# A 3x3 convolution in fp32 on one Trainium2 core: Winograd blocks of 2x2 outputs become blocks of 2x4, two images at a time

## The chip, the cores and the metric

The kernel runs on one core of a Trainium2 chip. The metric is the device time of one execution in microseconds. A core has a matrix engine (PE; its weight loads are listed apart, as PEld), a vector engine (DVE), a scalar engine (ACT), a general-purpose engine (POOL), and DMA queues that SP and POOL issue. Each engine works off its own list of instructions in order and waits for the others by semaphores.

## What is computed

The input x has 4 images of 1024 channels on a 32x32 grid (1024 positions), all fp32. Layer 0 is an attention block: q, k and v by 1024x1024 projections, rotary embedding and RMS norm of q and k, 16 heads of 64, softmax over the 1024 positions, an output projection, RMS norm, and the residual. Layer 1 is a bottleneck block, each batch norm over all 4 images and all positions of a channel:

```python
out = relu(bn(conv(x, w1, b1, 1, 0)))    # 1x1, 1024 -> 256
out = relu(bn(conv(out, w2, b2, 1, 1)))  # 3x3, 256 -> 256, pad 1
out = bn(conv(out, w3, b3, 1, 0))        # 1x1, 256 -> 1024
out = softplus(residual_scale)[0] * out
return relu(x + out)
```

The change concerns the 3x3 convolution, called conv2 here; its neighbours are conv1 and conv3.

## The kernel before

All four images are worked one after the other through projections and attention. Attention of an image goes by two chunks of 512 query positions and, in each, by eight pairs of heads. For a pair, PE computes eight score tiles (L789), ACT takes their exponentials (L796), DVE adds these up for the softmax's denominators (L815), PE multiplies them with v (L824), and ACT copies the context out (L830). Three PSUM banks hold scores. After the last pair come the denominators (L893, copied at L962, reciprocal at L963, sent through DRAM and multiplied into the contexts at L769, L770), then the output projection (L490, copied out at L544), whose weight chunks SP's queue loads into a ring of eight tiles.

Work of the next stage is slipped into the last attention chunk. `filters()` (L1145) turns the 3x3 filters into Winograd filters in a list of steps, and one step is issued after each head pair of that chunk, from the second pair on. On an engine's list a step so stands ahead of the next pair's exponentials and additions. Before the change the steps are the load, three sums along one direction, and two along the other (each with one ACT scaling of 1024 elements, L1166, between DVE operations L1165 to L1168). The 16 transformed filters stay in SBUF.

conv1 (L1013, and `conv1_first`/`conv1_rest`, L1054) is a 1x1 convolution. For images 0 to 2 it is done with a Strassen-like scheme in `conv1_rest`, a generator whose steps are interleaved by hand; for image 3 directly. Results go to DRAM (`h1d`), their statistics to `h1stats`, and `norm_of` (L1119 to L1126) makes scale and shift of the norm.

conv2 is a Winograd F(2x2, 3x3). A block of 2x2 outputs needs a 4x4 patch of inputs, transformed to 16 values; each of the 16 is multiplied over the channels, and four outputs come from them. So it has 16 products for 4 outputs, in place of 36. An image is loaded (`load_h1`, L1437), normed and clipped by ACT into a padded tile (`fill`, L1440), transformed by DVE across (`across`) and down (`down`, both L1451) into V tiles, multiplied by PE (`uv`, L1516, tiles of 256 blocks), copied in part by ACT (`copies`, L1531) and combined by DVE (`outputs`, L1539 to L1551) with bn_stats (L1553). The transform of the next image is interleaved with the products of this one. After the last image comes the norm of conv2 (L1558 on ACT, L1559 and L1560 on DVE). conv3's four weight tiles (`w3t`) and the residual x1 (`load_x1`) are loaded during conv2; conv3 is at L1656, with the copy L1667, statistics L1669, and the finish L1636 to L1640.

The order on PE, DVE, ACT and POOL is that of the program's lines, by hand; SP's queue of loads is ordered by the scheduler. PSUM banks, the V tiles, a ring of small work tiles (`temp`), one of larger ones (`big_temp`) and a ring of weight chunks (`chunk`) are shared, and an instruction that writes a shared buffer waits for its last reader.

Of the kernel before, what the change touches and what calls it, by code (L numbers as in the profile page):

```python
# [18 lines left out]
P = 128  # L19
B, C, H, W = 4, 1024, 32, 32  # L20
N = H * W
# [64 lines left out]
def program(ctx, tc, x, wblk, w2, w3, vecs, cos, sin, out, bad):  # L86
# [70 lines left out]
    wd2 = dram.tile([4, len(OUTER), len(SUMS), P, CH], F32, name=f"wd2{u}")  # L157
    dens = dram.tile([P, CH], F32, name=f"dens{u}")
# [4 lines left out]
    with tc.tile_pool(name=f"st{u}", bufs=2) as st, ExitStack() as s:  # L163
# [912 lines left out]
        def conv1_rest(b, ys, w, ss, t1, t2):  # L1076
# [13 lines left out]
            four(o, ss[2], lambda i: ys[:, i, half[1]], False, False)  # L1090
            h22 = temp(f"c22_{b}")
            nc.scalar.copy(h22, o)

            def done22():
                nc.vector.tensor_tensor(h22, h22, p5, ALU.add)
                keep_h1(b, 1, 1, h22)

            after(1, done22)
            product_done()
            yield  # L1100
            four(o2, ss[3], lambda i: ys[:, i + NH, half[1]], False, True)

            def done12():
                nc.vector.scalar_tensor_tensor(h12, o2, col("b1", 0), h12, ALU.add, ALU.add)
                keep_h1(b, 0, 1, h12)

            after(1, done12)
            product_done()
            yield
            four(o, w[1][1], lambda i: ys[:, i + NH, half[0]], False, True)  # L1110
# [36 lines left out]
        def filters():  # L1147
# [5 lines left out]
            def load():  # L1153
                for dy in range(3):
                    for dx, slot in enumerate((0, 1, 3)):
                        nc.gpsimd.dma_start(
                            raw[dy][:, slot, :].rearrange("p (c f) -> p c f", c=NPT), taps[:, :, 3 * dy + dx, :]
                        )

            steps.append(load)  # L1160
            two = [tp.tile([P, 2, CH], F32, tag=n, name=f"u2_{n}") for n in ("cos", "sin")]

            def sums_of(g0, g1, g2, new):

                nc.vector.tensor_tensor(new, g0, g2, ALU.add)  # L1165
                nc.scalar.mul(g1, g1, 0.5)  # L1166
                nc.vector.scalar_tensor_tensor(g1, new, 0.5, g1, ALU.mult, ALU.add)
                nc.vector.tensor_tensor(new, new, g1, ALU.subtract)  # L1168

            for dy in range(3):  # L1170
                r = raw[dy]
                steps.append(lambda r=r: sums_of(r[:, 0], r[:, 1], r[:, 3], r[:, 2]))
            for h in range(2):
                js = slice(2 * h, 2 * h + 2)
                steps.append(lambda h=h, js=js: sums_of(*(raw[dy][:, js] for dy in range(3)), two[h]))
            for i in range(4):
                for j in range(4):
                    uw[i, j] = two[j // 2][:, j % 2] if i == 2 else raw[(0, 1, None, 2)[i]][:, j]
# [218 lines left out]
        for b, nxt in ((1, 2), (2, 0), (0, None)):  # L1397
            steps = conv1_rest(b, back[b], w, ss, rows1, rows2)
            for _ in range(2):
                next(steps)  # L1400
            if nxt is not None:
# [10 lines left out]
        rest()  # L1412
# [11 lines left out]
        inner.close()  # L1424
        vp = s.enter_context(tc.tile_pool(name=f"vp{u}", bufs=1, reuse_waits="tile"))
        hx = s.enter_context(tc.tile_pool(name=f"hx{u}", bufs=3, reuse_waits="tile"))
        pad = [vp.tile([P, H + 2, W + 2], F32, name=f"pad{i}") for i in range(NPT)]
        cols = vp.tile([P, 4, H + 2, W // 2], F32, name="cols")
        for i in range(NPT):
            nc.gpsimd.memset(pad[i], 0.0)  # L1430
        TR, TC = H // 2, W // 2
        n1, n2, vt, h1, h2 = {}, {}, {}, {}, {}

        def load_h1(b):
            for i in range(NPT):
# [319 lines left out]
```

## Time and profile before

| | |
|---|---|
| median of 3 runs | 2645.34 us (2644.81 to 2646.97) |
| the profiled execution | 2645.64 us |
| its span, first to last instruction | 2643.8 us |
| PE busy | 2624.5 us (99%) |
| DVE busy | 2136.3 us (81%) |
| ACT busy | 1128.4 us (43%) |
| POOL busy | 451.9 us (17%) |
| granted PE clock | 0.998 |
| output projection of the last image begins | 2220.9 us |
| conv1 begins | 2305.6 us |
| conv2 begins | 2406.0 us |
| conv3 begins | 2518.4 us, its second half of channels (k=1) some 7.5 us later |
| last product of conv3 | 2628.8 us |

Positions are microseconds from the start of the span. A row of the groups names the line of the kernel, the engine, the operation, output and input with their shapes, and the count; then the busy time and the mean length of one in ns; then the idle time of the engine just ahead of these instructions and what ended it. A PE product in fp32 leaves two records. The records of operations that follow each other on an engine overlap a little, so a sum over many is made with the distance from start to start, which is less than the length.

### The profile page before, as it was taken

The page shows a single profiled execution, that of the slowest core. Times are in us where ns is not written, and L with a number is a line of the kernel's source. Part 1 is how long each engine was busy: PE and PEld are TensorE (multiplying, and loading weights), DVE is VectorE, ACT ScalarE, POOL GpSimd, SP SyncE. Part 2 cuts the span into 40 slices and gives each one's busy share as a digit, 9 for nine tenths or more (in the row PEclk, how much of TensorE's full clock was granted, in tenths as well). Part 3 has the DMA queues.
Part 4 walks back from the last instruction along what each step waited for, and adds up shares of the span by engine and source line. Part 5 has one row for each costly group of instructions (what it writes and reads, how often), then busy time and mean ns, then how long its engine had stood idle before and what let it go on. Part 6 is the DMA issues. An engine that isn't in the chain of part 4 may idle for free. (4 is left out here: it accounts for less than half of the span.)

```text
span 2643.8 us, 40486 instructions
## 1 busy us (share of the span) xinstructions
PE 2624.5 (99%) x15436; PEld 1628.9 (62%) x15436; DVE 2136.3 (81%) x2566; ACT 1128.4 (43%) x1586; POOL 451.9 (17%) x590
## 2 busy tenths in 40 slices
PE   9999999999999999999999999999999999999997
PEld 4448533488888333688886333888884335846843
DVE  5567899998887876888879777977988779877977
ACT  2222566533442565333343655233525654312266
POOL 2542323101011222100111222000111222010000
PEclk9999999999999999999999999999999999999999
DMA  8887888777667453557775551765774442683165
GB/s 287 288 257 202 240 262 258 209 219 237 188 183 210 88 94 64 150 172 225 190 198 144 97 90 46 219 202 177 194 212 90 84 105 84 206 278 104 64 236 210
DMA packets 252810, 466.81 MB, mean 177 GB/s; under 512 B 31808, under 2 KB 124784, under 8 KB 252608
## 3 DMA queue, kind: packets, MB, share of 16 engines
q1 hardware_dynamic: 195728, 287.80, 35.4%
q0 software_dynamic: 48816, 159.54, 24.6%
q10 hardware_dynamic: 8064, 16.78, 1.8%
q8 instruction: 125, 2.05, 0.3%
q14 instruction: 77, 0.63, 0.1%
HBM read 329.53 MB, written 97.01 MB: 161 GB/s over the span
## 5 line engine op out<-in xcount | busy, mean ns | idle before, releaser
L796 ACT ACTIVATE p<-sc 128x1024 f32<-128x1024 f32 x512 | 479.8, 1049 | 15.4 <-PE sc L789 15.1
L789 PE MATMUL sc<-q,k 64*64 64x512 f32 x4096 | 455.5, 591 | 0.0
L824 PE MATMUL cx<-p,to 64*64 64x512 f32 x3072 | 338.2, 589 | 0.0
L789 PEld LDWEIGHTS sc<-q,k 64*64 64x64 f32 x4096 | 149.7, 132 | 293.4 <-ACT p L796 148.0
L815 DVE TENSOR_TENSOR den<-den,p 128x1024 f32<-128x1024 f32 x192 | 237.9, 1239 | 21.9 <-ACT p L796 2.2
L815 DVE TENSOR_TENSOR den_T<-den_T,p 128x1024 f32<-128x1024 f32 x192 | 236.3, 1231 | 20.4 <-DVE den_T L815 1.4
L824 PEld LDWEIGHTS cx<-p,to 64*64 64x64 f32 x3072 | 117.5, 133 | 212.1 <-issue 211.0
L485 PE MATMUL p_v<-w_v,x 128*128 128x256 f32 x928 | 210.5, 379 | 1.7 <-DVE x L456 1.5
L490 PE MATMUL p_y<-q,w_y 128*128 128x256 f32 x928 | 210.6, 380 | 0.8 <-issue 0.8
L490 PEld LDWEIGHTS p_y<-q,w_y 128*128 128x128 f32 x928 | 175.7, 190 | 30.3 <-issue 5.8
L485 PEld LDWEIGHTS p_v<-w_v,x 128*128 128x128 f32 x928 | 176.0, 190 | 27.5 <-DVE x L456 2.8
L830 ACT COPY q<-cx 128x512 f32<-128x512 f32 x64 | 37.5, 585 | 341.1 <-PE cx L824 341.1
L490 PE MATMUL p_k<-to,w_k 128*128 128x256 f32 x672 | 152.2, 380 | 0.0
L490 PE MATMUL p_q<-to,w_q 128*128 128x256 f32 x672 | 152.2, 379 | 0.0
L490 PEld LDWEIGHTS p_k<-to,w_k 128*128 128x128 f32 x672 | 127.4, 190 | 18.4 <-issue 1.2
L490 PEld LDWEIGHTS p_q<-to,w_q 128*128 128x128 f32 x672 | 127.4, 190 | 18.4 <-issue 1.2
L770 POOL TENSOR_SCALAR q<-q,vec 128x512 f32<-128x512 f32 x42 | 80.5, 1926 | 215.6 <-DVE q L769 215.6
L824 PE MATMUL cx<-p,rq 64*64 64x512 f32 x1024 | 112.7, 589 | 0.0
L1656 PE MATMUL c<-h,w 128*128 128x512 f32 x256 | 110.3, 593 | 0.5 <-ACT h L1558 0.5
L485 PE MATMUL p_v<-w_v,t 128*128 128x256 f32 x384 | 90.1, 379 | 0.0
L490 PE MATMUL p_y<-to,w_y 128*128 128x256 f32 x384 | 90.1, 379 | 0.0
L732 POOL DMA_DIRECT2D k<-ks x64 | 57.6, 1087 | 180.2 <-ACT p L796 71.3
(509 smaller groups left out, 4323.1 us busy)
## 6 DMA issues: line engine op xcount, KB each, us to landing
w_v<-wd2f SPq DMA_DIRECT2D x112, 256.0 KB
w_y<-wd2f SPq DMA_DIRECT2D x112, 256.0 KB
w_q<-wd2f SPq DMA_DIRECT2D x84, 256.0 KB
w_k<-wd2f SPq DMA_DIRECT2D x84, 256.0 KB
wd2f<-w_pre POOLq DMA_DIRECT2D x68, 256.0 KB, 3.9
q<-qs POOLq DMA_DIRECT2D x64, 256.0 KB, 5.5
k<-ks POOLq DMA_DIRECT2D x64, 256.0 KB, 4.7
x1df<-y POOLq DMA_DIRECT2D x32, 512.0 KB, 5.6
```

What stands on the lines that cost most here:

```text
L485: nc.tensor.matmul(o[:, q].rearrange("p (g f) -> p g f", g=2), r[:, i, q * P : (q + 1) * P], wt[:, :, i, :], skip_group_check=True, **at,)
L490: nc.tensor.matmul(o[:, q], wt[:, q, i, :], r[:, i, :], skip_group_check=True, **at)
L732: nc.gpsimd.dma_start(dst[i::2, f, :], other[1 - i :: 2, :], accum_op=ALU.add)
L770: engine.tensor_scalar(cx, cx, col("bv", hp), None, ALU.add)
L789: nc.tensor.matmul(sc[keys, j], k_all[d, hp, t * P + keys.start : t * P + keys.stop], q_all[d, hp, at], start=True, stop=bad is not None,)
L796: nc.scalar.activation(p, sc, AF.Exp)
L815: nc.vector.tensor_tensor(d_, d_, p, ALU.add)
L824: nc.tensor.matmul(o[j * HD : (j + 1) * HD, i], v[keys, t, h0 : h0 + HD], probs[t][keys, j], start=(t == 0), stop=(t == N // P - 1),)
L830: nc.scalar.copy(cx, o[:, 0])
L1656: nc.tensor.matmul(os[i], w3t[k][f // NH][:, f % NH, :], h2[b, k][:, half[c]], start=(k == 0), stop=(k == NPT - 1),)
```

## The change

conv2 becomes a Winograd scheme with blocks of 2 rows by 4 columns: 4 values down, 6 across, 24 products for 8 outputs. Two images are worked at once, (1, 2) and then (0, 3), so that a tile still has 256 blocks. The six columns come in three groups of two (`GROUPS`), and for each group, output half and member there is one tile in a PSUM bank: over both image pairs 24 tiles, called by their number in `ks`, each with eight products.

- `filters()` has seven steps: load, two sums, the third sum with `fours`, `twos`, `ones_first`, `ones_last`. `twos` makes eight filter tiles that go to DRAM (`u34d`) in the chunk ring by eight POOL DMAs, and are read back by eight others when conv2 begins.
- The inputs are transformed by `first_cols`, `other_cols` and `down`. `keep` evacuates a bank by two ACT operations, `take` adds the rest of it on DVE, `outputs` combines them.
- The statistics of the first image pair go from DVE's bn_stats to 32 ACT operations with an accumulated output (`act_statistics`).
- In conv1, the last image of the scheme (0) and image 3 are reordered: image 3's first half of channels is done before image 0's last products, and those in the order fourth, third. The norm and the transform of the first half of channels lie under the rest of conv1; the first loads of `h1` for it are on POOL's queue.
- conv3's weights are one load of 1 MB after the last product of conv2, into the room of a V tile, and x1 has three homes instead of four.

The diff, cut; removed functions are those of the listing above.

```diff
+    u34d = dram.tile([2, 4, P, CH], F32, name=f"u34d{u}")
...
-        def conv1_rest(b, ys, w, ss, t1, t2):
+        def conv1_rest(b, ys, w, ss, t1, t2, early=False):
...
+            for step in (fourth, third) if early else (third, fourth):
+                step()
+                yield
...
-                for dy in range(3):
-                    for dx, slot in enumerate((0, 1, 3)):
+                for dx in range(3):
+                    for dy, slot in enumerate((0, 1, 3)):
                         nc.gpsimd.dma_start(
-                            raw[dy][:, slot, :].rearrange("p (c f) -> p c f", c=NPT), taps[:, :, 3 * dy + dx, :]
+                            raw[dx][:, slot, :].rearrange("p (c f) -> p c f", c=NPT), taps[:, :, 3 * dy + dx, :]
...
+            def down_sums(dx):
+
+                g0, g1, new, g2 = (raw[dx][:, i] for i in range(4))
                 nc.vector.tensor_tensor(new, g0, g2, ALU.add)
                 nc.scalar.mul(g1, g1, 0.5)
                 nc.vector.scalar_tensor_tensor(g1, new, 0.5, g1, ALU.mult, ALU.add)
                 nc.vector.tensor_tensor(new, new, g1, ALU.subtract)
 
...
+            def fours():
                 for j in range(4):
...
+                    t = flat(chunk(f"u3_{j}"))
+                    nc.vector.scalar_tensor_tensor(t, raw[2][:, j], 4.0, raw[0][:, j], ALU.mult, ALU.add)
+                    plus.append(t)
+
+            def twos():
+                for j in range(4):
+                    t = flat(chunk(f"u4_{j}"))
+                    nc.vector.scalar_tensor_tensor(t, raw[1][:, j], -2.0, plus[j], ALU.mult, ALU.add)
+                    nc.vector.scalar_tensor_tensor(plus[j], raw[1][:, j], 2.0, plus[j], ALU.mult, ALU.add)
+                    minus.append(t)
+                for i, ts_ in enumerate((plus, minus)):
+                    for j, t in enumerate(ts_):
+                        nc.scalar.mul(t, t, 1.0 / 24.0)
+                        nc.gpsimd.dma_start(u34d[i, j], t)
+
+            def ones_first():
+                for h in range(2):
+                    js = slice(2 * h, 2 * h + 2)
+                    nc.vector.tensor_tensor(two[h], raw[0][:, js], raw[2][:, js], ALU.add)
+                    nc.vector.tensor_tensor(raw[1][:, js], two[h], raw[1][:, js], ALU.subtract)
+
+            def ones_last():
+                for h in range(2):
+                    js = slice(2 * h, 2 * h + 2)
+                    nc.vector.scalar_tensor_tensor(two[h], two[h], 2.0, raw[1][:, js], ALU.mult, ALU.subtract)
+                    nc.scalar.mul(raw[0][:, js], raw[0][:, js], 0.25)
+                    nc.scalar.mul(raw[1][:, js], raw[1][:, js], -1.0 / 6.0)
+                    nc.scalar.mul(two[h], two[h], -1.0 / 6.0)
+
+            steps.append(load)
+            steps.append(lambda: down_sums(0))
+            steps.append(lambda: down_sums(2))
+            steps.append(lambda: (down_sums(1), fours()))
+            steps.append(twos)
+            steps.append(ones_first)
+            steps.append(ones_last)
...
-            for _ in range(2):
+            steps = conv1_rest(b, back[b], w, ss, rows1, rows2, nxt is None)
+            for _ in range(2 if nxt is not None else 3):
                 next(steps)
+            if nxt is None:
+                last_steps = steps
+                break
...
+        for c in range(NCH):
+            conv1(B - 1, 0, c, w, yt[B - 1], (lambda: norm1(0)) if c == NCH - 1 else None)
+        product_done()
+        for _ in range(2):
+            next(last_steps)
...
+        PAIRS, GROUPS = ((1, 2), (0, 3)), ((1, 2), (3, 4), (0, 5))
...
+        def fill(p, s_, i):
+            b = PAIRS[p][s_]
             nc.scalar.activation(
...
+                pads[s_][:, :, 1 : W + 1], h1[b, i].rearrange("p (a c) -> p a c", a=H), AF.Relu,
                 bias=n1[i][1], scale=n1[i][0],
             )
 
...
+        def columns(t):
+            return t.rearrange("p r (c q) -> p q r c", q=4)
+
+        def first_cols(i, which=range(2)):
+
+            efs = {}
+            for s_ in which:
+                ef = efs[s_] = temp(f"ef_{s_}_{i}").rearrange("p (x r c) -> p x r c", x=2, r=H)
+                for x in range(2):
+                    d, ahead_ = (columns(pads[s_][:, :, at : at + W])[:, x] for at in (1, 3))
+                    nc.vector.scalar_tensor_tensor(ef[:, x], d, -4.0, ahead_, ALU.mult, ALU.add)
+            for s_ in which:
+                for a, op in enumerate((ALU.add, ALU.subtract)):
+                    nc.vector.tensor_tensor(cols[:, i, a, s_, 1 : H + 1, :], efs[s_][:, 1], efs[s_][:, 0], op)
+
+        def other_cols(s_, i):
+
+            pad, d = pads[s_], steps_of
+            nc.vector.tensor_tensor(d, columns(pad[:, :, 2 : W + 2]), columns(pad[:, :, :W]), ALU.subtract)
+            for a, by in ((2, 2.0), (3, -2.0)):
+                nc.vector.scalar_tensor_tensor(
+                    cols[:, i, a, s_, 1 : H + 1, :], d[:, 1], by, d[:, 2], ALU.mult, ALU.add
+                )
+            nc.vector.scalar_tensor_tensor(
+                cols[:, i, 4:6, s_, 1 : H + 1, :], d[:, 0:2], -4.0, d[:, 2:4], ALU.mult, ALU.add
+            )
+
+        def down(p, i, g, js=range(4)):
+
+            c = cols[:, i, 2 * g : 2 * g + 2].rearrange("p a b (r q) c -> p q (a b) r c", q=2)
+            d0, d1, d2, d3 = (c[:, k % 2, :, k // 2 : k // 2 + TR] for k in range(4))
+            for j in js:
+                l, r, op = (
+                    (d0, d2, ALU.subtract), (d1, d2, ALU.add), (d1, d2, ALU.subtract), (d3, d1, ALU.subtract)
+                )[j]
+                out_ = v_tile(p, g)[:, i, j].rearrange("p a b (r c) -> p (a b) r c", r=TR)
+                nc.vector.tensor_tensor(out_, l, r, op)
...
+        for b in PAIRS[0]:
+            load_h1(b, 0, nc.gpsimd)
+        for s_ in range(2):
+            fill(0, s_, 0)
+        first_cols(0)
+        down(0, 0, 0, (1, 2))
+        for _ in last_steps:
+            pass
+        for b in PAIRS[0]:
+            load_h1(b, 1)
+        other_cols(0, 0)
+        conv1(B - 1, 1, 0, w, yt[B - 1])
+        other_cols(1, 0)
+        down(0, 0, 1, (1, 2))
+        conv1(B - 1, 1, 1, w, yt[B - 1], lambda: norm1(1))
+        down(0, 0, 0, (0, 3))
+        down(0, 0, 1, (0, 3))
...
+        u34 = [(a, j) for a, js in ((3, (1, 2)), (4, (0, 3, 1, 2)), (3, (0, 3))) for j in js]
+        for a, j in u34:
+            uw[a, j] = flat(chunk(f"u_{a}_{j}"))
+        for a, j in u34[:2] + u34[4:] + u34[2:4]:
+            nc.gpsimd.dma_start(uw[a, j], u34d[a - 3, j])
+        for s_ in range(2):
+            fill(0, s_, 1)
+        for b in PAIRS[1]:
+            load_h1(b, 0)
...
+            nc.scalar.mul(rows[:, 0], y, -1.0)
+            nc.scalar.copy(rows[:, 1], x)
+
+        def take(p, g, f):
+            for al in range(2):
+                m = mt[p, g, f, al].rearrange("p (r q c) -> p r q c", q=2, c=TC)
+                o = banks[p, g, f, al].rearrange("p (q r c) -> p r q c", q=2, c=TC)
+                nc.vector.tensor_tensor(m, o, m, ALU.add)
...
+            if g == 0:
+                sd = sums2[p, f] = acc.tile([P, 2, CH], F32, tag="tot", name=f"sd_{p}_{f}")
+                for i, op in enumerate((ALU.add, ALU.subtract)):
+                    nc.vector.scalar_tensor_tensor(sd[:, i], m0, col("b2", f), m1, ALU.add, op)
+                return
+            s0, d0 = (sums2[p, f][:, i] for i in range(2))
+            if g == 1:
+                s1 = temp(f"s1_{p}_{f}")
+                nc.vector.tensor_tensor(s1, m0, m1, ALU.add)
+                nc.vector.tensor_tensor(m0, m0, m1, ALU.subtract)
+                nc.vector.scalar_tensor_tensor(y[:, 2], grid(s1), 4.0, grid(s0), ALU.mult, ALU.add)
+                nc.vector.scalar_tensor_tensor(y[:, 1], grid(m0), 2.0, grid(d0), ALU.mult, ALU.add)
+                nc.vector.tensor_tensor(s0, s0, s1, ALU.add)
+                nc.vector.scalar_tensor_tensor(d0, m0, 8.0, d0, ALU.mult, ALU.add)
+                return
+            nc.vector.tensor_tensor(y[:, 0], grid(m0), grid(s0), ALU.add)
+            nc.vector.tensor_tensor(y[:, 3], grid(m1), grid(d0), ALU.add)
...
+            for i in range(8):
+                y = h2_all[:, f * B + i // 4, i % 4 * QT : (i % 4 + 1) * QT]
+                rest_ = temp(f"rest_{f}_{i}")[:, :QT]
+                nc.scalar.activation(rest_, y, AF.Identity, scale=1.0 / QT, accum_out=rec[:, i, 1:2])
+                nc.scalar.activation(rest_, y, AF.Square, bias=rec[:, i, 1:2], scale=-1.0, accum_out=rec[:, i, 2:3])
...
+        for k in ks[:8]:
+            products(k, 0, 0)
+        first_cols(1)
+        down(0, 1, 0)
+        for s_ in range(2):
+            other_cols(s_, 1)
+        down(0, 1, 1)
+        for s_ in range(2):
+            fill(1, s_, 0)
+        for b in PAIRS[1]:
+            load_h1(b, 1)
+        for i in range(NPT):
+            down(0, i, 2)
+        run((0, 5))
+        take(0, 0, 0)
+        take(0, 0, 1)
+        first_cols(0)
+        for s_ in range(2):
+            other_cols(s_, 0)
+        run((5, 9))
+        for s_ in range(2):
+            fill(1, s_, 1)
+        first_cols(1)
+        for i in range(NPT):
+            down(1, i, 0, (1, 2))
+        for i in range(NPT):
+            down(1, i, 0, (0, 3))
+        take(0, 1, 0)
+        take(0, 1, 1)
+        for s_ in range(2):
+            other_cols(s_, 1)
+        for i in range(NPT):
+            down(1, i, 1, (1, 2))
+        run((9, 13))
+        for i in range(NPT):
+            down(1, i, 1, (0, 3))
+        take(0, 2, 0)
+        take(0, 2, 1)
+        for i in range(NPT):
+            down(1, i, 2, (1, 2))
+        for i in range(NPT):
+            down(1, i, 2, (0, 3))
+        for g in range(3):
             for f in range(NPT):
...
+                outputs(0, g, f)
+        run((13, 17))
+        take(1, 0, 0)
+        run((17, 19))
+        act_statistics(0)
+        take(1, 1, 0)
+        outputs(1, 0, 0)
+        outputs(1, 1, 0)
+        run((19, 21))
+        act_statistics(1)
+        take(1, 2, 0)
+        take(1, 0, 1)
+        outputs(1, 2, 0)
+        outputs(1, 0, 1)
+        statistics(0)
+        run((21, 24))
+        norm2(0)
+        take(1, 1, 1)
+        outputs(1, 1, 1)
+        drain()
+        w3t_ = vp.tile([P, NPT, NT // NH, NH, P], F32, tag="V0", name="w3t")
+        w3t = [[w3t_[:, k, g] for g in range(NT // NH)] for k in range(NPT)]
+        nc.sync.dma_start(w3t_.rearrange("p k g i f -> p (k g i f)"), w3)
```

## The prediction

> **What bounds the kernel now.** I read the page first, then busy time by stage from the last attention chunk on (the change touches nothing earlier), then DVE's and ACT's rows and order of time in those stages.
>
> ```profile
> span 2643.8 us, 40486 instructions
> PE 2624.5 (99%) x15436; PEld 1628.9 (62%) x15436; DVE 2136.3 (81%) x2566; ACT 1128.4 (43%) x1586; POOL 451.9 (17%) x590
> PEclk9999999999999999999999999999999999999999
> ```
>
> PE is busy for 99% of the span, so a PE cycle removed is worth its length only if nothing else comes last in its place, and a stall given to PE is paid in full.
>
> ```profile
> 2183.00:2220.00 37.00, 37.00 (x344) 11.93 (x340) 35.06 (x33) 20.81 (x25) 7.95 (x4) 1.00 0.07 16
> 2406.00:2519.00 113.00, 112.99 (x516) 94.73 (x515) 104.49 (x156) 30.22 (x45) 0.00 (x0) 1.00 0.23 78
> 2629.00:2644.00 15.00, 0.38 (x1) 0.00 (x0) 7.60 (x14) 6.65 (x11) 0.00 (x0) 0.63 0.48 179
> ```
>
> Columns: stretch, its length, busy time of PE, PEld, DVE, ACT and POOL, granted clock, DMA share, GB/s. The first is the end of attention, the second the 3x3 convolution (conv2), the third the tail. In conv2 PE has no gap, but DVE is at 104.5 of 113 us: taking PE work out uncovers DVE almost at once. The end of attention is as full: DVE 35.1 of 37.
>
> **Part 1, what is saved on PE.** One 128x256 product is two records; the pairs of conv2 start every 0.4325 us (256 pairs, 110.7 us).
>
> ```profile
> L1516 PE MATMUL c2x<-V,t_w 128*128 128x256 f32 x192 | 53.0, 384 | 0.0
> L1516 PE MATMUL c2y<-V,t_w 128*128 128x256 f32 x192 | 51.9, 379 | 0.0
> ```
>
> After, there are 192 pairs (24 tiles, 8 pairs each), of the same 128x256 shape: 64 x 0.4325 = **-27.7 us**, if PE stays the bound of the stage. Attention, conv1 and conv3 keep their products.
>
> **Part 2, the filters in the last attention chunk.** Each step of the filter preparation is issued after a head pair, on ACT ahead of the next pair's exps. Before, a pair carried one 1024-wide ACT scaling:
>
> ```profile
> 2190.87 0.58 ACT L830 COPY q<-cx 128x512 f32<-128x512 f32 x1 [5.33 <-PE cx L824]
> 2191.35 1.06 ACT L1166 ACTIVATE t_w<-t_w 128x1024 f32<-128x1024 f32 x1
> 2192.31 1.93 ACT L796 ACTIVATE p<-sc 128x1024 f32<-128x1024 f32 x2
> ...
> 2206.24 1.06 ACT L1166 ACTIVATE t_w<-t_w 128x1024 f32<-128x1024 f32 x1
> 2207.20 3.76 ACT L796 ACTIVATE p<-sc 128x1024 f32<-128x1024 f32 x4
> ```
>
> How much PE forgives is visible here: the pair at 2206 took 7.33 us of scores instead of 6.87, so 1.06 us of ACT cost 0.46; some 0.6 us are free (three score banks), everything above is a stall.
> After, the step `twos` behind pair 5 (counted from 0) puts 8 scalar_tensor_tensor of 512 on DVE and 8 scalings of 512 on ACT, each waiting for its DVE operation; the fifth to last scaling needs the last DVE result. DVE reaches them after the four means (end 2192.2), plus up to 2.7 us for the four operations of `fours` one pair earlier, of which its thin idle time takes little. DVE's 512-wide scalar_tensor_tensor start 0.67 us apart: 8 x 0.67 = 5.4, so 2197.6 to 2200.3. Five scalings (row 632 ns, about 0.55 apart) are 2.7: the exps of pair 6, all queued behind, begin at 2200.3 to 2203.0 instead of 2192.3. Less 0.6: a PE stall of 7.4 to 10.1; I take **+9**. The 8 writes of these tiles to DRAM on POOL's queue wait for the same scalings; POOL's only work there, 7.95 us of scaling, is ahead of them. 2 MB in a stretch with a DMA share of 0.07 is hidden. SP's first eight loads of the projection's weights stand behind these writes (shared tiles): by my reckoning they land at 2203 to 2213, needed from about 2230; nothing lost, a few us if the writes were 15 us later.
> `ones_last` behind the last pair puts six 1024-wide scalings ahead of the copies that free the banks of the denominators and of the first projection products:
>
> ```profile
> 2221.00 0.59 ACT L962 COPY rec<-dn 128x512 f32<-128x512 f32 x1 [0.46 <-PE dn L893]
> 2222.91 0.58 ACT L544 COPY y<-p_y 128x512 f32<-128x512 f32 x1 [1.33 <-PE p_y L490]
> ```
>
> Six at 0.96 apart are 5.8, with up to 2.4 for the two DVE operations some wait for, and about 1.3 free (the idle time before the second copy): 4.4 to 8.7 with the later chain reciprocal, DMA, means; I take **+6**.
>
> **Part 3, conv1's end.** Reordering moves two products and puts half the channels' transform under conv1. Same products, other order; two waits for copies in the new order, about +1 (0 to 2).
>
> **Part 4, conv2 counted on DVE.** By the rows, start to start: 512-wide tensor_tensor 0.61, 1024-wide 1.135, scalar_tensor_tensor 512 0.67, and 256-wide about 0.36 and 0.42 (the one row: 421 ns).
>
> ```profile
> L1451 DVE TENSOR_TENSOR V<-cols 128x1024 f32<-128x1024 f32 x26 | 30.1, 1216 | 0.0
> L1549 DVE SCALAR_TENSOR_TENSOR y<-n,vec,n 128x512 f32<-128x512 f32 x16 | 12.0, 748 | 0.3
> L1451 DVE TENSOR_TENSOR V<-cols 128x256 f32<-128x256 f32 x8 | 3.0, 421 | 0.1
> ```
>
> After: 48 `down` of 512: 29.3; columns, four times (3.1 + 2 x 2.65): 33.4; 24 `take` of 512: 14.6; outputs, four times (5 x 0.67 + 5 x 0.61): 26; eight bn_stats 4.9; two norms 6. Sum 114. The old transform, outputs, statistics and norms add up to 116 the same way. So the cheaper product gives DVE no less to do, and only some 13 us of it (before 8) lie under conv1: **DVE becomes the bound**, with about 101 us after conv1 against PE's 83.
> On top come waits that the order makes. (a) ACT's fill of the next images stands ahead of the first evacuations and waits until DVE has read the padded tiles: PE waits some 5 us for a bank at the start. (b) The evacuation of the 15th tile needs a buffer that is free only after the outputs of the first image pair, 76 us of DVE's list; PE stops there some 18 us. Both are the DVE bound made visible, not additional. (c) Additional are DVE's own idle times: 32 ACT statistics operations of 128x256 with an accumulator, 16 in a row twice, whose temporaries share a ring with DVE's tiles (about 9 us), and the root of the first norm behind an evacuation (6 us). From conv1's end to the second half of conv3: 101 + 9 + 6 + 2 (wait for a fill) + 3 (start after the norm) + 7 (last products and norm) = 128, before 120.3: **+7.6** in place of -27.7.
> The accumulating form is in no row. From below: copy rows of 585 ns (512) and 1049 (1024) give 0.40 at 256; from above 0.9, two passes. I take 0.55; the ends move the sum by -4 and +10.
> Moved with it: the loads of conv1's result on POOL's queue (POOL 0.00 busy in conv2) and 2 MB of filters read back (DMA share 0.23) are hidden. conv3's weights as one 1 MB load after the last product instead of four loads during conv2: at the stage's own 224 GB/s of conv3 it is 5 us, just before the first product that needs it; 0 to +4, I take +2 with three x1 homes instead of four.
>
> **The clock gate, row against rule.** The row 2629 to 2644 shows a granted clock of 0.63 once PE is idle, 1.00 in all others. The Trainium skill, "TensorE: Matmul & The Clock Gate", Part 1, has the clock fall to half after about 3.4 us without work and stay there until about 3.4 us of work are done. It speaks against this change: five gaps above 3.4 us (9, 6, 5, 18, 4) are new. By the trace alone, where no gap precedes work, they cost nothing more; by the rule each costs about 1.7 us, 8.5 in all, of which the three in conv2 lie under the DVE bound: estimate +3. I take +2.
>
> **Sum.** 9 + 6 + 1 + 7.6 + 2 + 2 = +27.6. The profiled run took 2645.64, 1.8 outside its span, 0.3 above the median of the runs: 2645.3 + 28 = **2673**.
>
> **Rivals.**
> *Faster (0.09).* conv2 becomes PE-bound after all. The place is DVE's list between conv1 and conv3, the price -27.7 + 16 (parts 2, 3) + 4 (conv3's weights, clock) = -7.7, 2638. The other parts cost 20 us, so it decides at a stretch of 95 us in place of my 128: every DVE operation at three quarters of its row, or the statistics' idle time gone and more of the list under conv1. For it: ACT takes over statistics and is busy for only 27% of the stage. Against: rows for the 512-wide forms exist, and the new operands have shorter inner rows (8 elements instead of 16), which is no reason for speed.
> *A small loss (0.14).* Parts 2 and 3 as said, but the idle times of (c) don't come, since ACT's accumulation is short: conv2 breaks even or gains 7: +10 to +18, 2655 to 2663.
> *A larger loss (0.12).* Accumulations at 0.9 and a cold clock after each gap: +10 and +6, 2690 and above.
> *Nothing moves (0.03).* The filter stalls alone hide in slack that I don't see.
> *The forecast (0.62):* 2663 to 2690.
>
> **From this.** Within 0.2% (5 us) is what a measurement can't tell from no change. Faster 0.09, same 0.03, slower 0.88. Range 2655 to 2691: below it 0.12, above it 0.08.
>
> **What would show it.** PE: 384 records in conv2, and gaps before the scores of pair 6 (9 us), before the y projection (6), and 18 us around the 15th tile; DVE above 90% busy in conv2; the granted clock below 1.00 beside the gaps. The prediction fails if the exps of pair 6 start before 2196 (then ACT's order is not what I read), if PE runs through conv2 in about 90 us, or if the 128x256 accumulations take over 0.7 us.

## The result and the profile after

The changed kernel takes 2693.6 us (median of 4 runs, 2690.1 to 2693.9) against 2646.0 of the kernel before beside it: a ratio of 1.0177, 95% interval 1.016 to 1.0195, so 1.8% slower. The forecast had the sign, but 28 us of loss where 48 came, and 2693.6 lies 2.6 us above its range, which ended at 2691.

The page of the changed kernel:

```profile
span 2691.7 us, 40390 instructions
PE 2611.6 (97%) x15308; PEld 1613.5 (60%) x15308; DVE 2152.3 (80%) x2601; ACT 1151.5 (43%) x1678; POOL 462.7 (17%) x610
PEclk9999999999999999999999999999999999999899
```

PE has 128 records less, and yet it is busy for only 12.9 us less, not 27.7: some of its products were slower. The rest is new idle time. The order of time on PE shows the gaps (start, length, and in brackets the idle time before and who ended it):

```profile
2207.24 6.86 PE L790 MATMUL sc<-q,k 64*64 64x512 f32 x48 [11.22 <-ACT p L797]
...
2243.47 3.75 PE L491 MATMUL p_y<-q,w_y 128*128 128x256 f32 x8 [5.85 <-issue]
...
2393.97 5.40 PE L1055 MATMUL c1s<-back,c_S 128*128 128x512 f32 x8 [2.56 <-ACT c1p L1088]
...
2453.54 1.22 PE L1590 MATMUL c<-V,u_cos 128*128 128x256 f32 x2 [5.03 <-ACT h L1640]
...
2521.36 3.44 PE L1590 MATMUL c<-V,u 128*128 128x256 f32 x8 [19.43 <-ACT m L1640]
...
2543.01 1.99 PE L1590 MATMUL c<-V,t_w 128*128 128x256 f32 x8 [2.68 <-ACT m L1640]
...
2553.39 1.99 PE L1590 MATMUL c<-V,u 128*128 128x256 f32 x8 [3.21 <-ACT m L1640]
...
2572.57 104.71 PE L1829 MATMUL c<-h,w3t 128*128 128x512 f32 x240 [5.14 <-ACT h L1699]
```

With three others (0.68, 3.20 and 1.37) these gaps add up to 60.4 us. Behind a gap the products are slow: 48 score records take 6.86 us where 5.38 is usual for the 48 of one pair, eight records of p_y 3.75 instead of 1.89, eight of conv1 5.40 instead of 3.60. Where the 48 us went, by stage (positions of the two profiled executions):

| stage | before | after | difference | forecast |
|---|---|---|---|---|
| everything ahead of the last attention chunk (to 2076 us, unchanged) | 2076.2 | 2078.7 | +2.5 | 0 |
| from there to conv1 (last attention pairs, projection) | 229.4 | 249.9 | +20.5 | +15 |
| conv1 | 100.4 | 106.1 | +5.7 | +1 |
| conv2's first product to conv3's second half | 120.1 | 137.9 | +17.8 | +7.6 |
| conv3's second half to the end | 117.7 | 119.1 | +1.4 | +2 |

The forecast's other 2 us, for the clock, had no stage of their own. The 2.5 us ahead of the change are drift and nothing that the change does: over the twelve kernels profiled here, all the same up to that point, it lies at 2075.8 to 2081.0. Stages are therefore compared below from one product to another, not by spans.

### The profile page after: what moved, and what is told of

Same layout as the page of the kernel before. It is cut to its first block, busy times and chain, and to the rows that moved or that the text cites. A ratio compares the mean times of both kernels' runs of the same rounds, so it can differ in the third digit from the quotient of the medians.

```text
span 2691.7 us, 40390 instructions
## 1 busy us (share of the span) xinstructions
PE 2611.6 (97%) x15308; PEld 1613.5 (60%) x15308; DVE 2152.3 (80%) x2601; ACT 1151.5 (43%) x1678; POOL 462.7 (17%) x610
## 5 line engine op out<-in xcount | busy, mean ns | idle before, releaser
L797 ACT ACTIVATE p<-sc 128x1024 f32<-128x1024 f32 x512 | 479.9, 1048 | 17.1 <-PE sc L790 16.8
L790 PE MATMUL sc<-q,k 64*64 64x512 f32 x4096 | 456.7, 592 | 11.2 <-ACT p L797 11.2
L1829 PE MATMUL c<-h,w3t 128*128 128x512 f32 x256 | 111.7, 599 | 5.1 <-ACT h L1699 5.1
L1829 PEld LDWEIGHTS c<-h,w3t 128*128 128x128 f32 x256 | 49.2, 192 | 67.1 <-issue 55.7
```

The costliest lines, as they stand in the source:

```text
L790: nc.tensor.matmul(sc[keys, j], k_all[d, hp, t * P + keys.start : t * P + keys.stop], q_all[d, hp, at], start=True, stop=bad is not None,)
L797: nc.scalar.activation(p, sc, AF.Exp)
L1829: nc.tensor.matmul(os[i], w3t[k][f // NH][:, f % NH, :], h2[b, k][:, half[c]], start=(k == 0), stop=(k == NPT - 1),)
```

## The experiments

All are edits of the changed kernel, at 2693.6 us, unless another one is named.

### Attention: ACT's scalings, or DVE's operations?

`fold` drops the 14 scalings of filter tiles on ACT. Their factors go into constants that are there anyway: the outputs carry -6 times the convolution, which the norm takes out.

```diff
-                        nc.scalar.mul(t, t, 1.0 / 24.0)
...
-                    nc.scalar.mul(raw[0][:, js], raw[0][:, js], 0.25)
-                    nc.scalar.mul(raw[1][:, js], raw[1][:, js], -1.0 / 6.0)
-                    nc.scalar.mul(two[h], two[h], -1.0 / 6.0)
```

> The changed kernel without the 14 scalings of filter tiles on ACT (8 in twos, 6 in ones_last); their factors sit in the constants of the output combinations and in the norm, no operation added. Theory A (ACT's order holds PE up, and each gap of PE costs some 1.8 us of half clock behind it): the gaps of 11.2 us before the scores of pair 6 and of 5.8 us in the y projection go, with 1.7 and 1.9 us of slow products: 20.6 us less, about 2673. Rival B (the twelve operations on DVE hold it up, not ACT): the first gap stays at 6 us or more, the time is 2681 or above.

2687.7 us (ratio to the kernel before 1.0156, 1.0139 to 1.0173): 6 us less, not 20. The waits of PE from the last chunk into the projection, by line and engine waited for (total, times, longest), of this kernel:

```profile
PE cx L825 <- DVE q L900: 8.0, 2, 5.2
PE p_y L491 <- PE p_y L491: 0.8, 1, 0.8
PE p_y L491 <- DVE q L900: 0.7, 1, 0.7
```

ACT no longer holds PE up; now DVE does, at L900, where it takes a context out of the only bank for contexts. But the two gaps, 2.85 and 5.17 us, have different causes. Ahead of the first, DVE works without a pause, and L900 stands behind the eight operations of `twos`: this gap is the new work on DVE, as rival B had it. Ahead of the second, DVE itself stands still for longer than PE does (first line: SP's queue, who it waited for, in total, times, longest; then the order of time):

```profile
SPq L389 <- DMA u34df<-u: 24.1, 3, 23.5
2213.48 0.54 SPq L938 DMA_DIRECT2D densf<-rec  x1
2219.33 0.25 DVE L954 RECIPROCAL few<-few 128x16 f32<-128x16 f32 x1 [5.48 <-DMA few<-densf]
2224.51 0.68 DVE L900 TENSOR_TENSOR q<-q,cx 128x512 f32<-128x512 f32 x1
2225.24 8.43 PE L825 MATMUL cx<-p,to 64*64 64x512 f32 x64 [5.17 <-DVE q L900]
```

DVE waits at L954 for a softmax denominator that comes back from DRAM. Its transfer (L938) is issued by SP's queue, behind loads of projection weights, and these wait for the writes of the filter tiles (`u34df`) to leave the tiles that they share. In the kernel before, the same transfer went out at 2194.7 us, ahead of all these loads; here at 2213.5. Without those 5.48 us of idle time, more than PE's gap of 5.17, L900 would have come before PE needed it (an estimate from these two numbers). So theory A's place was right and its size wrong: behind ACT stood DVE, and behind DVE the queue of loads. From the last chunk to conv1 the time falls from 249.9 to 242.7 us, and 13.3 of the 20.5 us stay, the slow products behind the two new gaps among them.

`late` goes on from there: no scaling, and the two `ones` steps move into conv1, the rest spread over pairs 2 to 6.

```diff
-            steps.append(lambda: down_sums(0))
-            steps.append(lambda: down_sums(2))
-            steps.append(lambda: (down_sums(1), fours()))
-            steps.append(twos)
-            steps.append(ones_first)
-            steps.append(ones_last)
+            steps.append(lambda: (down_sums(0), down_sums(2)))
+            steps.append(lambda: down_sums(1))
+            steps.append(fours)
+            steps.append(lambda: twos((0, 1)))
+            steps.append(lambda: twos((2, 3)))
+            ones_steps.extend([ones_first, ones_last])
```

> The kernel without the 14 scalings, and further: ones_first and ones_last are issued in conv1 instead of behind pairs 6 and 7, twos in two halves behind pairs 5 and 6, fours behind pair 4, the three sums behind pairs 2 and 3. Theory A (in the last attention chunk DVE has no room: the 8 us of its twelve new operations came back as gaps of 2.9 and 5.2 us before context products, with slow products behind each): both gaps go, 10 us less than without the scalings alone, 2677 to 2680. Rival B (conv1 has no room on DVE either, or the weights of the projection come late because of the later writes): gaps of the same size there, 2685 or more.

2677.3 us (1.0117, 1.01 to 1.0134). PE has no gap left there, and from the last chunk to conv1 it takes 229.4 us, as before the change. So all of the 20.5 us are accounted for by the filters' new work and its writes, at a place without room. The expectation put both gaps of `fold` down to DVE; this run can't tell, for it moves DVE's work and also the order on SP's queue (the transfer of the denominators is again issued ahead of the loads, at 2196.5 us). conv1 lost some (110.1 us instead of 106.1): its gap before `fourth` grew from 2.56 to 5.60.

### The slow products behind a gap

`warm` fills two gaps with 12 and 6 products that nobody reads, in the idle half of the bank of the denominators.

```diff
...
+            for _ in range({f"{B - 1}_1_5": 12, f"{B - 1}_1_7": 6}.get(n, 0)):
+                nc.tensor.matmul(other, ones, sums_[0][:, 0], start=True, stop=True)
```

> The changed kernel with 12 and 6 products of 128x512 that nobody reads, written to the unused half of the bank of two denominators: they lie in the PE gaps before the scores of pair 6 (11.2 us) and in the y projection (5.8 us). Theory A (the clock falls in a gap, and the products behind it run at half clock for some 3.4 us): the 48 score records behind the first gap take 5.2 us instead of 6.86, the 8 behind the second 1.9 instead of 3.75: 3 to 3.6 us less, 2690. Rival B (these products are slow for another reason, their operands or the semaphores): they stay slow, 2693.6 or more.

2690.4 us (1.0167, 1.015 to 1.0184). The same score and projection records, behind filled gaps:

```profile
2205.21 5.43 PE L790 MATMUL sc<-q,k 64*64 64x512 f32 x48 [0.71 <-ACT p L797]
2241.53 1.97 PE L491 MATMUL p_y<-q,w_y 128*128 128x256 f32 x8 [2.20 <-issue]
```

6.86 became 5.43, 3.75 became 1.97: the records are slow because PE stood still ahead of them, not because of what they are. Of the 3.2 us won, 2.1 remain from the last chunk to conv1: the second gap ends no earlier than it did (164.9 us into the stretch, 164.8 in the changed kernel), so what was won behind the first gap was lost again there. The other 1.2 us of the median are not told from the drift of the unchanged part. The changed kernel's stretches say the same by the granted clock (the second number from the left is the length, the next one PE's busy time, the clock the third from the right):

```profile
2243.00:2248.00 5.00, 4.53 (x11) 3.68 (x12) 4.49 (x3) 0.86 (x2) 0.62 (x1) 0.52 0.00 0
2393.00:2400.00 7.00, 6.03 (x10) 2.60 (x11) 0.54 (x1) 0.69 (x1) 1.67 (x5) 0.76 1.03 411
2434.60:2560.40 125.80, 90.89 (x388) 76.14 (x387) 100.42 (x164) 40.97 (x123) 0.54 (x1) 0.89 0.18 56
```

The first stretch is the projection just behind its gap: 0.52, half clock. In conv2, the last line, which ends with its last product, PE is busy for 91 us with products that take 83 at full clock.

### conv2: DVE's strided operands

The rows of DVE in the changed kernel that bear on it:

```profile
L1532 DVE TENSOR_TENSOR steps<-pad 128x1024 f32<-128x1024 f32 x8 | 16.3, 2036 | 0.1
L1524 DVE SCALAR_TENSOR_TENSOR ef<-pad 128x256 f32<-128x256 f32 x16 | 9.0, 623 | 0.2 <-ACT pad L1509 0.2
L1534 DVE SCALAR_TENSOR_TENSOR cols<-steps 128x256 f32<-128x256 f32 x16 | 6.1, 422 | 0.3
L1675 DVE TENSOR_TENSOR h<-m,sd 128x512 f32<-128x512 f32 x4 | 4.4, 1096 | 0.0
L1671 DVE TENSOR_TENSOR sd<-sd,s 128x512 f32<-128x512 f32 x4 | 2.8, 696 | 0.0
```

The same operation and size takes 623 or 422 ns, 1096 or 696, 2036 where 1216 was the row before: the slow ones read the padded tile, or write h, at every fourth element. The kernel before read its padded tile at every second element, and that cost nothing: 717 ns for 544 elements, where contiguous rows of 512 took 684 to 696:

```profile
L1451 DVE TENSOR_TENSOR cols<-pad 128x544 f32<-128x544 f32 x28 | 18.6, 717 | 1.4 <-ACT pad L1440 1.4
```

`planes` stores the padded tile as four planes, so that DVE reads neighbours and ACT's fill does the striding.

```diff
-                pads[s_][:, :, 1 : W + 1], h1[b, i].rearrange("p (a c) -> p a c", a=H), AF.Relu,
+                pads[s_][:, :, :, :TC], h1[b, i].rearrange("p (a k r) -> p r a k", a=H, r=4), AF.Relu,
```

> The changed kernel with the padded tiles stored as four planes (every fourth column together), so that first_cols and other_cols read runs of 8 neighbouring elements instead of every fourth; ACT's fill reads every fourth element instead. Theory A (DVE is the bound of conv2, and its reads at a stride of four elements are what the forecast missed): steps falls from 2.05 to 1.33 us (three operations) and ef from 0.62 to 0.42, 9 us of DVE in all, some 7 behind conv1: 2685 to 2688. Rival B (the stage is bound by ACT and by PE's slow clock): the time stays within 2 us of 2693.6. Rival C: ACT's strided read takes what DVE gains: fill above 2 us instead of 1.27, and the gap at the start of conv2 grows.

2694.1 us (1.018, 1.0163 to 1.0197): nothing gained. DVE's and ACT's rows of this kernel:

```profile
L1529 DVE SCALAR_TENSOR_TENSOR ef<-pad 128x256 f32<-128x256 f32 x16 | 6.0, 420 | 8.5 <-ACT pad L1509 8.5
L1538 DVE TENSOR_TENSOR steps<-pad 128x512 f32<-128x512 f32 x8 | 5.5, 682 | 0.0
```

```profile
L1509 ACT ACTIVATE pad<-h1l,sh,sc 128x1024 f32<-128x1024 f32 x8 | 17.8, 2262 | 7.4 <-DVE steps L1541 6.5 <-DVE sh L1133 0.9
```

Rival C it was, though at another place than it said. DVE's reads became fast (623 to 420 ns, and 682 + 2 x 417 for the 2036), and ACT's fill, 1271 ns before, now takes 2262. In conv2 DVE has 7.0 us less work (105.0 instead of 112.0 us) and waits 8.5 us for the fills, since they stand directly ahead of their readers; the stage stays at 137.9.

`noperm` leaves out the interleaving of the four output columns: they are written as contiguous blocks, so that conv3 sees the positions in another order (the result is that of permuted positions; the time is what counts here).

```diff
-            y = flat2(h2_all[:, at, :]).rearrange("p (r c o) -> p o r c", c=TC, o=4)
+            y = flat2(h2_all[:, at, :]).rearrange("p (o r c) -> p o r c", c=TC, o=4)
```

> The changed kernel without the interleaving of the four columns: outputs writes each of them as one contiguous block, so conv3 gets the positions in another order and the result is that of permuted positions; every operation and shape stays. Theory A (DVE writes at a stride of four elements at 1.09 us for 512 instead of 0.69, and the stage waits for DVE): 16 writes 0.4 us shorter, the gap at tile 14 shrinks from 19.4 by 3.2 (eight of them lie in it), 3 to 6 us less in all, 2687 to 2690. Rival B (the stride costs nothing in the write, it is the two reads from different rings): the writes stay at 1.09 and the time at 2693.6.

2689.0 us (1.0162, 1.0145 to 1.0179), 4.6 us less. The writes of h are fast now, 682 ns where they took 1096:

```profile
L1675 DVE TENSOR_TENSOR h<-m,sd 128x512 f32<-128x512 f32 x4 | 2.7, 682 | 0.0
```

Strided writes cost too, as A had it. By the stage it is less than by the median: in the profiled run, the slowest of the four, conv2 takes 135.2 instead of 137.9, and the gap at tile 14 is 17.54 instead of 19.43.

### conv2: the ring of larger tiles, and ACT's statistics

`hxbuf` puts tiles 14 to 17 into two tiles that are idle by then.

```diff
-                    mt[p, g, f] = big_temp(f"m_{p}_{g}_{f}")
+                    if (p, f) == (1, 0) and g > 0:
+                        mt[p, g, f] = hx.tile([P, N], F32, tag="hx", name=f"m_{p}_{g}_{f}")
+                    else:
+                        mt[p, g, f] = big_temp(f"m_{p}_{g}_{f}")
```

> The changed kernel with one edit: the evacuations of groups 1 and 2 of the first output half in the second image pair (tiles 14 to 17) go to the two tiles of the h1 loads, which nobody needs by then, instead of the ring of three larger tiles. Theory A (PE's gap of 19.4 us at tile 14 is the wait for a ring tile, and since DVE idles some 20 us later in the stage, filling the gap shortens the stage): the gap falls below 6 us and the time by 8 to 15, 2679 to 2686. Rival B (DVE's list is the bound from end to end): the gap only moves to tile 18, less than 3 us gained, 2691 or more.

2677.9 us (1.0122, 1.0105 to 1.0139). The gap of 19.43 us is gone; the next one, at tile 18, is

```profile
2518.70 1.22 PE L1590 MATMUL c<-V,u_cos 128*128 128x256 f32 x2 [5.36 <-ACT m L1643]
```

and conv2 takes 122.7 us instead of 137.9. DVE's work in the stage is the same (first the changed kernel, then `hxbuf`, then `best1` of the next part; DVE is the third busy time):

```profile
2434.60:2572.57 137.97, 97.92 (x404) 78.99 (x403) 111.95 (x184) 45.17 (x128) 0.54 (x1) 0.90 0.22 73
2433.30:2556.02 122.72, 98.55 (x402) 78.98 (x400) 111.84 (x184) 45.18 (x128) 0.54 (x1) 0.91 0.24 82
2408.78:2531.01 122.23, 98.55 (x403) 78.66 (x401) 116.35 (x191) 29.58 (x64) 0.54 (x1) 0.91 0.24 82
```

Theory A is right, and with it the forecast's sentence on this gap ("the DVE bound made visible, not additional") is wrong: by two tiles of 4 KB in each partition 15 us come back without any work less on DVE. PE stood still while DVE worked, and then DVE stood still while PE and ACT caught up: DVE's idle time falls from 26 to 11 us, and its wait of 9.0 us for ACT's statistics to 0.5.

`bnstats` returns the first pair's statistics to DVE.

```diff
         def act_statistics(f):
 
+            for s_ in range(2):
+                for c in range(NCH):
+                    nc.vector.bn_stats(h2stats[:, f, 2 * s_ + c, :], h2_all[:, f * B + s_, half[c]])
+
+        def unused_statistics(f):
+
...
```

> The changed kernel with the statistics of the first image pair by 8 bn_stats on DVE in place of 32 accumulating operations on ACT. Theory A (ACT's two blocks of 8 us stop DVE for 9.0 and 5.8 us and PE for 2.7 and 3.2): DVE has 4.9 us more work and 12 or more less idle time; 5 to 9 us less, 2685 to 2689. Rival B (DVE is the bound throughout, the idle time moves elsewhere): 0 to 5 us more.

2686.9 us (1.0149, 1.0132 to 1.0166), conv2 131.5 us instead of 137.9, as theory A had it: more work on DVE (116.6 us instead of 112.0 in the stage), and less time. In the changed kernel these operations on ACT, which were in no row before, are:

```profile
L1690 ACT ACTIVATE rest<-h,h2stats 128x256 f32<-128x256 f32 x16 | 8.1, 508 | 0.5
L1689 ACT ACTIVATE rest<-h 128x256 f32<-128x256 f32 x16 | 6.5, 404 | 0.0
L1689 ACT ACTIVATION_READ_ACCUMULATOR rest<-h 128x1 f32 x16 | 3.0, 189 | 0.0
L1690 ACT ACTIVATION_READ_ACCUMULATOR rest<-h,h2stats 128x1 f32 x16 | 3.0, 187 | 0.0
```

Each operation has a second instruction that reads the accumulator. By lengths that is 593 and 695 ns; start to start, one after the other, 0.52 us, 8.3 us for each block of 16. DVE waited 9.0 us for the first block. Its wait of 5.8 us was for the root of the norm, which stood on ACT behind an evacuation, as the forecast had it.

### All together, and further

`best1` is `late`, `bnstats` and `hxbuf`, and in conv1 image 3's first product goes between image 0's second and fourth, which share a bank.

> All together: without the scalings, steps moved as in late, bn_stats for both image pairs, tiles 14 to 17 in the tiles of the h1 loads, and in conv1 image 3's first product put between image 0's second and fourth, which use one bank (a gap of 2.5 us and slow products behind it). Theory A (the causes add): 2693.6 - 20.6 - 6.5 - 12 - 4.4 = 2650. Rival B (what conv2 gives is bound by DVE's list, so that the last two overlap): 2658 to 2668.

2653.1 us (1.0028, 1.0016 to 1.0039), 40.5 us less. By themselves the parts gave 16.3 (late), 6.7 (bnstats), 15.7 (hxbuf), and the gap in conv1 with its slow products 4.4, which is 43.1 in all. That the two sums are near each other is in part chance. By stage, `late` had won 20.5 us and lost 4.0 in conv1, which comes back here too (101.6 us). And in conv2 `hxbuf` alone had won 15.2 us and `bnstats` 6.4, but both together win 15.7 (122.2 us): there they overlap, as rival B had it. DVE is busy for 116 of these 122 us (the third line above): only now is DVE's list the bound of the stage from end to end.

`best2` therefore takes work off DVE: the planes, the fills moved so that ACT does them while DVE has other work, and half of the first pair's statistics on ACT, two at a time between evacuations. `best2n` is the same without the planes. From the diff of `best2`:

```diff
+        for i in range(NPT):
+            down(0, i, 2)
+        run((0, 3))
         for s_ in range(2):
             fill(1, s_, 0)
         for b in PAIRS[1]:
             load_h1(b, 1)
-        for i in range(NPT):
-            down(0, i, 2)
-        run((0, 5))
+        run((3, 5))
...
-        first_cols(1)
-        for i in range(NPT):
-            down(1, i, 0, (1, 2))
-        for i in range(NPT):
-            down(1, i, 0, (0, 3))
+        down(1, 0, 0, (1, 2))
+        down(1, 0, 0, (0, 3))
         take(0, 1, 0)
         take(0, 1, 1)
+        first_cols(1)
+        down(1, 1, 0, (1, 2))
+        down(1, 1, 0, (0, 3))
```

> best1 with three further edits: the padded tiles in four planes (as in planes, with the two first column operations of an image in one); the fills of the second pair's first half behind the third evacuation and DVE's order turned so that it has other work while ACT fills; the statistics of the first pair's first output half again on ACT, but two at a time between the evacuations. Theory A (conv2 is now DVE's list alone, 122 us of it; ACT has room): DVE loses 8.6 us of strided reads, 2.5 of statistics and 1 by merging, and waits some 2 us for fills: 10 us less than best1, 2643, below the kernel before. Rival B (ACT's fills at 2.26 us still stop DVE, as in planes): 2650 to 2653.

> best2 without the planes: best1 with the fills and DVE's order moved and the statistics of one half spread on ACT. Theory A (only DVE's amount of work counts): 2.5 us less than best1, 2650.5. Rival B (the gaps of PE at the start of conv2, 5.5 us and slow products, count): 5 to 8 us less, 2646.

`best2`: 2641.2 us, ratio to the kernel before 0.9982 (0.9975 to 0.9988). `best2n`: 2647.7 us, 1.0005 (0.9997 to 1.0013). conv2 takes 110.7 and 116.8 us, against 120.1 before the change. DVE in `best2`, and its fill on ACT:

```profile
2410.00:2520.00 110.00, 97.40 (x400) 78.70 (x399) 106.05 (x193) 42.76 (x95) 0.52 (x1) 0.94 0.26 91
```

```profile
L1518 ACT ACTIVATE pad<-h1l,sh,sc 128x1024 f32<-128x1024 f32 x7 | 15.7, 2288 | 0.9 <-DVE sh L1137 0.9
```

The fills are as slow as in `planes` (2288 ns), but DVE (106 of 110 us busy) now waits 1.4 us for them instead of 8.5. The planes were worth nothing where the slower fill stood on the path, and 6.1 us of conv2 where it was hidden (about 1 of them, as expected in advance, for two column operations made one). `best2n` lies between its two theories: 5.4 us of conv2 less than `best1`, more than DVE's 2.5. The kernel with 2x4 blocks, so rearranged, is 4.6 us faster than the kernel before (2641.2 against 2645.8 beside it), out of 27.7 that PE saves: DVE is still the bound of the stage. What such a rearrangement would give the kernel before was not tried.

## Why the prediction was right or wrong

The direction was right, and so were the places: PE stalls at the filters, and in conv2 it waits for DVE and ACT. What failed is the size of several terms, and that DVE's list already sets conv2's time. Of the 20 us that the forecast missed, conv2 has 10.2, the last attention chunk and projection 5.5, conv1 4.7, and 2.5 are drift; conv3 and the clock's own term give 2.6 back.

- **Part 1, 27.7 us on PE.** The count was right (384 records). It was right too that nothing of it arrives.
- **Part 2, +9 and +6.** The places, the engine and the releasing rows were right: 11.2 and 5.85 us. The first is larger because three of the scalar_tensor_tensor of `twos` took 1.06 us instead of 0.68, 1.1 us in all; the rest is that DVE came to them late, near the end of the range that the forecast gave. That ACT alone is the cause was wrong. Behind it stood DVE's new work (2.85 us in `fold`), which the prediction's own row, DVE at 35.1 of 37 us, had said; the prediction did not ask what remains once ACT is out of the way. And behind that stood SP's queue (the gap of 5.17 us in `fold`): the forecast saw the weights wait behind the filter writes and set it at "nothing lost", but the denominators' transfers are on the same queue.
- **Part 3, +1.** 3.2 us of gaps, and 1.8 of slow products. The new order puts `fourth` right behind the product whose bank it continues, and ACT's copy of that bank waits 4.6 us for the store of an older tile of its ring. "Two waits for copies" named it and priced it too low; `best1` takes it away with one product in between.
- **Part 4, +7.6.** 17.8. The step that failed is the list of DVE's durations: "256-wide about 0.36 and 0.42", "1024-wide 1.135", and 0.61 and 0.67 for all 512-wide operations were taken from rows with other strides. Start to start, steps took 2.05 (8 x 0.92 = 7.3 more), ef 0.54 (16 x 0.12 = 2), the writes of h 0.90 (16 x 0.27 = 4.3): 13.6 us on a list of 114. In the stage DVE was busy for 112 us where the forecast had 101, and idle for 26 where it had 27. That these 11 us are the 10.2 missed is this sum, not an experiment: 5.1 us of DVE work less gave 2.7 of conv2 (`noperm`), 7.0 less gave nothing while ACT paid for it (`planes`), and 6.1 once ACT's part was hidden (`best2` against `best2n`). The rivals' part looks at the length of the inner rows and not at the step between the elements. The Trainium skill speaks against the change just there ("SBUF — State Buffer", section "Door 1: The DMA port swizzle", the note on cachelines): lines of 16 bytes, of which two accesses each are needed for the full rate, so that fp32 at a stride of four elements falls off it. Every row here agrees, the stride of two in the kernel before, which costs nothing, included. The same note's "how far you can stride for free depends on dtype: 4 fp32" could be read as allowing a stride of four; the rows decide against that reading.
- The same part, **(b)**, "not additional": wrong, by `hxbuf`. The gap and DVE's later idle time were both in the list of waits, and each was explained by itself; together they are a buffer that is missing. With two tiles more, 15 us came back at the same 112 us of DVE work, so DVE was not yet the bound that "DVE becomes the bound" made it; it is in `best1`, at 116 of 122 us.
- The same part, **(c)**, 9 + 6: 9.0 and 5.8. The accumulating operation, taken at 0.55 us, took 0.52 start to start.
- **A sign that did not come.** "DVE above 90% busy in conv2" was 112 of 138 us, 81%. The forecast's own sum, 101 of 128 us, speaks against it too.
- **The clock, +2.** The row against rule was decided for too little. Ahead of conv2, where nothing lies over it, three gaps cost 1.5, 1.9 and 1.8 us, 5.1 in all, near the 1.7 each that the forecast had estimated from the Trainium skill's rule ("TensorE: Matmul & The Clock Gate", Part 1). The 3.4 us are no threshold for a gap, as the forecast read them: behind 2.56 us in conv1 the products were slow, behind 2.68 and 3.21 us in conv2 they were not (1.99 for eight records). The same page calls the window free-running, and the runs agree with that: the very gap of 2.67 us is followed by 3.78 for eight records in `fold` and `noperm`, and by 1.99 in `warm` and `planes`. In rows of 0.1 us, the changed kernel's clock stands at 0.50 for 3.4 us in conv1, 6.8 in the projection, 10.3 in attention and 17.1 around tile 14: once, twice, three and five times the same length.
- **The rest**, +2 for conv3's weights and x1: +1.4, of which the first products behind the gap of 5.14 us are the most.

By the sum: 60.4 us of gaps against 53.3 that the forecast's terms contain (9 + 6 + 1 + 2, and in conv2 27.7 + 7.6), and some 13 us of slow products (47.9 - 2.5 of drift - 60.4 + 27.7 + 0.5 of old gaps) against 2. Both missed terms point the same way, so the range, made of independent ends, was too narrow on that side.

## What to carry to other kernels

Before work is taken off the bound of a stage, list what the next engine has to do there, operation by operation, and look for a row with the same stride, not only the same size. A gap on one engine with a later gap on another, in the same stage, is a missing buffer and not a bound; one tile can be worth more than the arithmetic saved. And a wait that is taken away shows the next one behind it: look at every engine and every DMA queue in the stretch, not only at the one that released the wait.

## What the runs showed of the hardware

- fp32 on DVE at a stride of four elements: 2036 ns instead of 682 + 2 x 417 for 1024 elements read, 623 instead of 420 for 256, 1096 instead of 696 for a write of 512. ACT's fill of 1024 went from 1271 to 2262 ns when its input had that stride (and its output came in runs of eight elements instead of 32). The kernel before read its padded tile at a stride of two (128x544 in 717 ns), with no such loss.
- Three in-place scalar_tensor_tensor of 512 took 1.06 us each while POOL scaled tiles, and 0.69 when it had ended; those between them, with another output, took 0.68 all along. What sets this apart was not tried.
- Behind a gap of PE, products ran at half clock (0.50 granted in rows of 0.1 us) for 2.9 us (behind the gap of 19.43) to 6.0 us (behind 5.03) in the changed kernel, and products that nobody reads, put into the gap, prevented it (`warm`). Behind its gaps of 0.68, 2.68 and 3.21 us there was no half clock.
